# A first store in three transfers, a new list of slots, and one product that signals differently

## The chip, the cores and the metric

The kernel runs on one core of one Trainium2 chip. The metric is the device time of one execution in microseconds (us), given as the median of several runs. Beside it stands one profiled execution, with its own time and its span (from the first to the last instruction of the program).

## What is computed

The input `x` holds 4096 rows of 32 fields of 64 numbers (f32), and `W` is a 64 x 64 matrix. Each field is multiplied by `W`, and then each of the 496 pairs of fields i < j gives one product, number by number:

```python
vid = jnp.einsum('bfd,de->bfe', x, W)
idx_i, idx_j = jnp.triu_indices(F_, k=1)
return x[:, idx_i, :] * vid[:, idx_j, :]
```

So 33.6 MB are read and 4096 x 496 x 64 x 4 B = 520.1 MB are written.

## The kernel before

**Layout.** The two halves of the batch lie side by side on the 128 partitions (2 x 64 numbers of a field), so that a "unit" is one field or one product of a tile: 128 columns of 4 B, that is 512 B on each of 128 partitions, 64 KB in all. The batch is cut into 16 tiles of 128 columns; a tile has 32 fields (units) and 496 products (units). All units live in one SBUF tensor `mem` of 445 units. The output is a stream of 16 x 496 = 7936 products, in an order that `by_block` fixes.

**Work of a tile.** TensorE multiplies the fields by `W` (kept twice on the diagonal of `w2`) into PSUM (`vid`), in two halves of 16 fields: the high half (fields 16 to 31) first, then the low half (`half`, L305). VectorE (DVE) multiplies fields from `mem` with fields from `vid` and writes products back into `mem` (L285): first the pairs within the high half (64 + 32 + 16 + 8 products), then the 256 pairs across the halves, then those within the low half.

**Slots.** `SLOTS` cuts the stream into stores by hand. Each entry is (number of products, first unit in `mem`, seams): the products of a slot lie in consecutive units and leave in one DMA (`store`, L245, through `transfer`, L183, all issued by SyncE, SP). A seam is a place at which a product instruction is cut too, so that a part of a slot can be made before the rest of its units is free. `products` cuts the instructions at slots and seams. A unit may be written again when the store that reads it has landed and the products that read it are made; `after` collects these waits. The homes are so laid that slots reuse the units of older slots and of tiles that are used up. 74 slots make 270 product instructions.

**Loads.** The tiles come in two groups (`GROUPS`): tiles 0 to 7 and tiles 8 to 15. Tile 0 and `W` come first in two loads; then `load(0)` issues three loads of 128, 70 and 26 units. At tile 8, `load(1)` issues three loads of 102, 128 and 26 units over the places of the first group. SP is one queue: what is issued later waits behind what is issued earlier. The first store behind each set of loads also waits until the last but one of these loads has landed (`hold[-2]`). Slots from number `STRETCHES[0]` on are stored behind `load(1)`.

**Signals.** Each product instruction raises one semaphore: `made` (stores and loads wait for it) or `free` (TensorE waits for it before it overwrites a half of `vid`). The last product on a half should raise `free`; if it is the last of its slot it must raise `made`, and a later one raises `free`. For a product that raised `free`, `work` notes the next `made` as the one to wait for, so whoever needs that product waits for one product more.

Of the kernel before, what the change touches and what calls it, by code (L numbers as in the profile page):

```python
# [10 lines left out]
P = 128  # L11
# [10 lines left out]
    (0, [(96, 224), (26, 96), (0, 26)]),  # L22
    (8, [(154, 256), (26, 154), (0, 26)]),
]
STRETCHES = [37]


SLOTS = [
# [10 lines left out]
]  # L39


PAD = 24
# [9 lines left out]
def by_block():  # L52


    def within(lo, fields):
        n, many = fields // 2, 1
        while n:
            yield ((many, fields // many, 0), (n, 0, 1), (n, 1, 1)), lo, lo + fields - 2 * n + 1
            n, many = n // 2, many * 2

    yield from within(16, 16)
    yield ((1, 0, 0), (16, 0, 1), (16, 1, 0)), 0, 16
    yield from within(0, 16)


def products(blocks, at=0):

    for nest, i, j in blocks:
        units = [n for n in accumulate((n for n, _, _ in nest[:0:-1]), lambda a, b: a * b, initial=1)][::-1]
        r, size = 0, units[0] * nest[0][0]  # L70
        while r < size:
            room = min(BREAKS[bisect_right(BREAKS, at)] - at, size - r)
            level = next(k for k, unit in enumerate(units) if r % unit == 0 and room >= unit)
            count = nest[level][0]
            part = min(count - r // units[level] % count, room // units[level])
            places = [r // unit % n for unit, (n, _, _) in zip(units, nest)]
            yield (
                at,
                part * units[level],
                ((part, *nest[level][1:]), *nest[level + 1 :]),  # L80
                i + sum(k * di for k, (_, di, _) in zip(places, nest)),
                j + sum(k * dj for k, (_, _, dj) in zip(places, nest)),
            )
            at += part * units[level]
            r += part * units[level]
# [16 lines left out]
def fields(a, lo, steps, whole):  # L102


    first = a[:, lo : lo + 1, :]
    dims = [[step * C, n] for n, step in steps if n > 1 or whole]
    dims = [*dims[:-1], [1, dims[-1][1] * C]] if whole else [*dims, [1, C]]
    return bass.AP(first.tensor, first.offset, [list(first.ap[0]), *dims])
# [36 lines left out]
def place_of(t, fields):  # L145

    first = max(begin for begin, _ in GROUPS if begin <= t)
    return TOP - (t - first + 1) * fields
# [10 lines left out]
def pairwise_bilinear_kernel(nc, x0, x, out):  # L159
# [8 lines left out]
    mem = ctx.enter_context(nc.sbuf_tensor([P, UNITS, C], F32))  # L168
# [3 lines left out]
    made = nc.alloc_semaphore("made")  # L172
    free = nc.alloc_semaphore("free")
# [3 lines left out]
    sp, dve = Queue(nc.sync, behind), Queue(nc.vector, behind)  # L177
# [3 lines left out]
    def transfer(out_, in_, units, reads, needs):  # L181
        sem = nc.alloc_semaphore(f"moved{len(moved)}")
        sp.issue(lambda: nc.sync.dma_start(out=out_, in_=in_), needs).then_inc(sem, 16)  # L183
        sp.note(sem, 16)
        moved.append((units, reads, sem))
        return sem

    def after(units):

        needs = [(s, 16) for u, reads, s in moved if reads and overlap(u, units)]  # L190
        last = max((n for spans, n in worked if any(overlap(units, s) for s in spans)), default=0)
        return needs + [(made, last)] * (last > 0)

    counts = {made: 0, free: 0}

    def work(make, spans, needs, tells):


        instruction = dve.issue(make, needs)
        instruction.then_inc(tells, 1)  # L200
        counts[tells] += 1
        worked.append((spans, counts[made] + (tells is free)))
        dve.note(tells, counts[tells])
# [18 lines left out]
    owed = 0  # L222
# [3 lines left out]
    def load(g):  # L226
        (begin, pieces), end = GROUPS[g], ends(NT)[g]
        begin = max(begin, 1)
        low = place_of(end - 1, F)
        sems = []  # L230
        for lo, hi in pieces:
            at = (begin - 1) * F + lo - low
            sems.append(transfer(mem[:, lo:hi, :], x[:, at : at + hi - lo, :], (lo, hi), False, after((lo, hi))))
            loads.append((range(begin, end), (lo, hi), sems[-1]))
        return sems

    def loaded(t):
        units = (place_of(t, F), place_of(t, F) + F)
        return [(sem, 16) for tiles, piece, sem in loads if t in tiles and overlap(piece, units)]

    hold = load(0)
    begins = [begin for begin, _ in GROUPS]
    held = []

    def store(slot, last):  # L245
        nonlocal hold
        begin, end = STARTS[slot : slot + 2]
        home = SLOTS[slot][1]
        units = (home, home + end - begin)
        needs = [(made, last)]  # L250
        if hold:
            needs.append((hold[-2], 16))
            hold = []
        transfer(out[:, begin:end, :], mem[:, units[0] : units[1], :], units, True, needs)


    for t in range(NT):
        if t in begins[1:]:
            hold = load(begins.index(t))
            for late in held:  # L260
                store(*late)
            held = []
        xs = (place_of(t, F), place_of(t, F) + F)
        blocks = list(products(by_block(), t * NP))
        for k, (at, n, nest, i, j) in enumerate(blocks):
            slot = bisect_right(STARTS, at) - 1
            begin, end = STARTS[slot], STARTS[slot + 1]
            home = SLOTS[slot][1]
            units = (home + at - begin, home + at - begin + n)
            whole = nest[-1][1:] == (1, 1)  # L270
            inner = [n for n in accumulate((c for c, _, _ in nest[:0:-1]), lambda a, b: a * b, initial=1)][::-1]
            o = fields(mem, units[0], [(c, step) for (c, _, _), step in zip(nest, inner)], whole)
            left = fields(mem, xs[0] + i, [(c, step) for c, step, _ in nest], whole)
            right = fields(vid, j, [(c, step) for c, _, step in nest], whole)
            top = i + sum((c - 1) * step for c, step, _ in nest)
            high = j >= HALF
            later = blocks[k + 1 : k + 2]
            owed += not later or high and later[0][4] < HALF
            tells = free if owed and at + n < end else made
            owed -= tells is free  # L280
            needs = [(there, 2 * t + 2 - high), *after(units)]
            if tells is free and t + 1 < NT and t + 1 not in begins:
                needs += loaded(t + 1)
            work(
                lambda: nc.vector.tensor_tensor(o, left, right, ALU.mult),  # L285
                [units, (xs[0] + i, xs[0] + top + 1)],
                needs,
                tells,
            )
            at += n  # L290
            if at == end:
                late = (slot, counts[made])
                group = sum(behind <= slot for behind in STRETCHES)
                if t < begins[group]:
                    held.append(late)
                else:
                    store(*late)
# [63 lines left out]
```

## Time and profile before

| | |
|---|---|
| Time, median of 3 runs | 1284.66 us (1284.65 to 1284.83) |
| Time of the profiled execution | 1284.39 us |
| Its span | 1283.1 us |
| VectorE busy | 1079.9 us (84%) |
| TensorE busy | 182.7 us (14%) |
| DMA transfers | 8 loads, 74 stores |
| DMA packets | 11,812, 553.71 MB |

The span is 1.3 us shorter than the profiled execution's own time, and that is 0.3 us below the median. Busy shares are averages over the whole span. A DMA "packet" is one piece of a transfer as one of the 16 DMA engines carries it; "landing" is the moment at which the last engine has reported its part. A row of the windows view gives, for a stretch of time, the busy time and the number of instructions of each engine, the granted clock of TensorE, the share of time for which the 16 DMA engines had a packet, and the rate; packets count where they start, so that a short stretch can show more than its share.

### The profile page before, as it was taken

What the parts mean: (1) busy time and instruction counts of PE and PEld (TensorE: products, weight loads), DVE (VectorE), ACT (ScalarE), POOL (GpSimd) and SP (SyncE); (2) the same over time, 40 slices, a digit from 0 to 9 for tenths busy, and PEclk for the clock granted to TensorE, in tenths of its full rate; (3) what the DMA queues carried; (4) which work ended last, traced back from release to release, by engine and by line L of the source; (5) the groups of instructions that cost most, each with busy time, mean ns of one, the idle gap of its engine ahead of it and who ended that gap; (6) DMA issues with size and microseconds to landing.
All of it is one profiled execution on the core that took longest, in us unless ns stands there. A gap on an engine that the chain in (4) does not pass through costs nothing. (4 is left out here: it accounts for less than half of the span.)

```text
span 1283.1 us, 1255 instructions
## 1 busy us (share of the span) xinstructions
PE 182.7 (14%) x256; PEld 71.2 (6%) x256; DVE 1079.9 (84%) x273; POOL 0.2 (0%) x4
## 2 busy tenths in 40 slices
PE   3011120301221030300030112203030020201100
PEld 1000000100000010100010000001010010000000
DVE  5589989988897989998028989989998899899980
POOL 0000000000000000000000000000000000000000
PEclk8566565656556565655565665556565565756655
DMA  9999999999999999999999999999999999999999
GB/s 403 438 429 429 447 421 433 447 427 425 439 444 425 435 427 444 426 431 452 412 426 434 431 431 434 437 433 429 444 431 425 442 437 429 425 435 445 429 423 409
DMA packets 11812, 553.71 MB, mean 432 GB/s; under 512 B 1313, under 2 KB 1313, under 8 KB 1313
## 3 DMA queue, kind: packets, MB, share of 16 engines
q1 hardware_dynamic: 11808, 553.69, 100.0%
q14 instruction: 4, 0.02, 0.0%
HBM read 33.59 MB, written 520.09 MB: 432 GB/s over the span
## 5 line engine op out<-in xcount | busy, mean ns | idle before, releaser
L285 DVE TENSOR_TENSOR mem<-mem,vid 128x1024 f32<-128x1024 f32 (+11 forms) x270 | 1079.3, 4065 | 161.4 <-DMA out_dram<-mem 112.0
L305 PE MATMUL vid<-mem,w 128*128 x256 | 182.7, 881 | 1012.4 <-PEq L303 1012.4
L305 PEld LDWEIGHTS vid<-mem,w 128*128 128x128 f32 x256 | 71.2, 292 | 1123.1 <-issue 1123.1
L217 DVE COPY w<-mem 64x64 f32<-64x64 f32 x2 | 0.4, 189 | 5.2 <-DMA mem<-in_r_x_dram 5.2
L214 DVE MEMSET w<- 128x128 f32 x1 | 0.2, 165 | 0.8 <-PEq L330 0.8
L330 POOL MEMSET const-bfloat16-1.0<- 128x1 bf16 x1 | 0.1, 101 | 0.0
L330 POOL MEMSET const-uint8-127<- 128x1 uint8 x1 | 0.1, 101 | 0.0
L330 POOL MEMSET const-float32-0.0<- 128x1 f32 x1 | 0.1, 98 | 0.2 <-issue 0.2
L330 POOL MEMSET const-float32-1.0<- 128x1 f32 x1 | 0.1, 98 | 0.0
## 6 DMA issues: line engine op xcount, KB each, us to landing
out_dram<-mem SPq DMA_DIRECT2D x12, 7680.0 KB, 23.3
out_dram<-mem SPq DMA_DIRECT2D x5, 7168.0 KB, 22.0
out_dram<-mem SPq DMA_DIRECT2D x4, 6656.0 KB, 20.2
out_dram<-mem SPq DMA_DIRECT2D x6, 4096.0 KB, 17.5
out_dram<-mem SPq DMA_DIRECT2D x4, 5120.0 KB, 19.3
out_dram<-mem SPq DMA_DIRECT2D x3, 6144.0 KB, 20.3
out_dram<-mem SPq DMA_DIRECT2D x3, 5632.0 KB, 18.4
out_dram<-mem SPq DMA_DIRECT2D x2, 5440.0 KB, 19.6
```

The lines of the kernel that those rows point to most:

```text
L214: work(lambda: nc.vector.memset(w2[:, :], 0.0), [], [], made)
L217: lambda: nc.vector.tensor_copy(w2[half, half], mem[half, place + F, :D]),
L285: lambda: nc.vector.tensor_tensor(o, left, right, ALU.mult),
L305: last = nc.tensor.matmul(vid[:, b : b + BANK, :], lhsT=w2[:, :], rhs=xt(b), start=True, stop=True)
L330: nc = _bacc.Bacc("TRN2", target_bir_lowering=False, num_devices=1, dynamic_dma_scratch_size=512)
```

## The change

`SLOTS` is replaced: 75 slots in place of 74, all with new sizes and homes, and the first 38 (not 37) are stored ahead of `load(1)`. Slot 0 now has 28 products, and `PARTS` cuts its store by partitions: rows 0 to 111, 112 to 119 and 120 to 127 go in three transfers. The last product of tile 7, the last one ahead of the second group, now always raises `made`; an instruction of VectorE's sequencer behind it waits for that and raises `free`, so that the loads of the second group wait for this product and not for the next.

```diff
--- before.py
+++ after.py
@@ -22,21 +22,24 @@
     (0, [(96, 224), (26, 96), (0, 26)]),
     (8, [(154, 256), (26, 154), (0, 26)]),
 ]
-STRETCHES = [37]
+STRETCHES = [38]
 
 
 SLOTS = [
-    (80, 256), (109, 336), (83, 240, 16), (56, 323, 13), (64, 379), (80, 240), (56, 323), (64, 379),
-    (104, 224, 99), (117, 328, 51), (115, 208, 16), (96, 323, 5), (64, 192, 16), (88, 256, 67), (96, 344),
-    (112, 192, 64), (128, 304, 40), (128, 160, 32), (128, 288, 16), (128, 144, 16), (120, 272, 16), (80, 128, 16),
-    (104, 208, 64), (128, 312), (128, 112), (128, 240, 72), (128, 96), (128, 224, 16), (112, 80), (120, 192, 32),
-    (120, 312), (128, 48), (128, 176), (128, 304), (128, 32), (128, 160), (128, 304), (104, 256), (85, 360),
-    (51, 240, 16), (64, 291), (88, 355), (104, 240, 51), (88, 344, 11), (72, 224), (64, 296, 48), (85, 360),
-    (107, 224, 72), (112, 331, 29), (120, 192, 32), (120, 312, 19), (112, 176, 16), (64, 288, 24), (80, 352),
-    (128, 176), (128, 304, 48), (128, 144, 32), (128, 272), (120, 128, 16), (120, 248, 24), (96, 112, 16),
-    (112, 208, 40), (120, 320), (120, 112, 96), (128, 232, 88), (128, 80, 32), (128, 208, 24), (128, 48, 32),
-    (128, 176, 32), (120, 304), (120, 48), (128, 168), (128, 296), (120, 48),
+    (28, 256), (68, 284), (92, 352), (108, 240, 16, 44), (88, 348, 4), (60, 240), (68, 300), (76, 368), (76, 224),
+    (64, 300), (80, 364), (104, 224), (112, 328, 36), (120, 192), (116, 312, 16), (108, 176, 16), (64, 284, 28),
+    (96, 348), (128, 176), (128, 304, 44), (120, 144, 32), (128, 264, 40), (88, 128), (112, 216, 48), (112, 328),
+    (128, 128), (128, 256), (128, 80, 48), (128, 208, 48), (104, 336), (128, 80), (120, 208), (128, 48, 32),
+    (128, 176, 32), (128, 304), (128, 16), (128, 144), (116, 272), (100, 256), (88, 356), (52, 240, 16),
+    (76, 292, 64), (77, 368), (99, 240), (104, 339, 29), (72, 224), (80, 296, 43), (64, 376), (104, 224, 72),
+    (112, 328, 48), (120, 192), (116, 312, 16), (108, 176, 16), (96, 284, 28), (64, 380), (128, 176, 108),
+    (128, 304, 76), (120, 144, 32), (128, 264, 40), (88, 128), (112, 216, 48), (112, 328), (128, 112), (128, 240),
+    (128, 80, 32), (128, 208, 32), (104, 336), (128, 80), (120, 208), (128, 48, 32), (128, 176, 32), (128, 304),
+    (128, 16), (128, 144), (120, 272),
 ]
+
+
+PARTS = {0: [slice(0, 112), slice(112, 120), slice(120, 128)]}
 
 
 PAD = 24
@@ -251,7 +254,8 @@
         if hold:
             needs.append((hold[-2], 16))
             hold = []
-        transfer(out[:, begin:end, :], mem[:, units[0] : units[1], :], units, True, needs)
+        for rows in PARTS.get(slot, [slice(0, P)]):
+            transfer(out[rows, begin:end, :], mem[rows, units[0] : units[1], :], units, True, needs)
 
 
     for t in range(NT):
@@ -276,7 +280,8 @@
             high = j >= HALF
             later = blocks[k + 1 : k + 2]
             owed += not later or high and later[0][4] < HALF
-            tells = free if owed and at + n < end else made
+            last = not later and t + 1 in begins
+            tells = free if owed and at + n < end and not last else made
             owed -= tells is free
             needs = [(there, 2 * t + 2 - high), *after(units)]
             if tells is free and t + 1 < NT and t + 1 not in begins:
@@ -287,6 +292,11 @@
                 needs,
                 tells,
             )
+            if last:
+                nc.vector.wait_ge(made, counts[made]).then_inc(free, 1)
+                dve.learn({made.num: counts[made]})
+                counts[free] += 1
+                owed -= 1
             at += n
             if at == end:
                 late = (slot, counts[made])
```

## The prediction

> **What bounds the kernel now.** I read the page first: the span, the busy shares and the DMA rows.
>
> ```profile
> span 1283.1 us, 1255 instructions
> ## 1 busy us (share of the span) xinstructions
> PE 182.7 (14%) x256; PEld 71.2 (6%) x256; DVE 1079.9 (84%) x273; POOL 0.2 (0%) x4
> ...
> DMA packets 11812, 553.71 MB, mean 432 GB/s; under 512 B 1313, under 2 KB 1313, under 8 KB 1313
> ## 3 DMA queue, kind: packets, MB, share of 16 engines
> q1 hardware_dynamic: 11808, 553.69, 100.0%
> ```
>
> The 16 DMA engines hold a packet for 100.0% of the span, and the bytes are those of the input and the output (33.6 and 520.1 MB), so none can be saved. VectorE, at 84%, has slack. The packets tell how a transfer is dealt out. There are 82 transfers (8 loads, 74 stores); 1,312 of the small packets are 82 x 16, a completion from each of the 16 engines; the 10,496 large ones are 82 x 128, one for each partition row. So an engine carries 8 rows of a 128-row transfer.
>
> Then the windows view, by stage (columns: stretch and length; busy time and instructions of PE, PEld, DVE, POOL; granted clock; DMA share, GB/s), to see where time is not spent at full rate.
>
> ```profile
> 0.00:2.00 2.00, 0.00 (x0) 0.00 (x0) 0.17 (x1) 0.20 (x4) 1.00 0.41 59
> ```
>
> ```profile
> 2.00:42.00 40.00, 9.76 (x16) 3.93 (x16) 28.38 (x11) 0.00 (x0) 0.72 1.01 429
> 42.00:642.00 600.00, 82.08 (x112) 31.87 (x112) 511.53 (x126) 0.00 (x0) 0.56 1.00 433
> 642.00:682.00 40.00, 9.93 (x16) 4.05 (x16) 16.71 (x5) 0.00 (x0) 0.59 0.98 424
> 682.00:1282.00 600.00, 80.95 (x112) 31.34 (x112) 523.07 (x131) 0.00 (x0) 0.57 1.00 433
> ```
>
> Both long stretches of stores run at 433 GB/s, share 1.00: a plateau. 553.69 MB at 433 GB/s are 1278.7 us; the span holds 4.4 us more. The first 2 us move 0.12 MB, which loses 1.7 us; 40 us of loading at 429 lose 40 x 4/433 = 0.4 us; the second loading at 424 loses 40 x 9/433 = 0.8 us (a packet at an edge of these 40 us makes both figures rough); the remaining 1.5 us lie in rounding and in the tail. The first 2 us and the final report stay, so **all that any schedule could win is the two losses at the loads and part of the tail, under 2 us of 1283**. Being over 0.2% (2.6 us; about what a measurement of this kernel can tell from no change) faster is all but excluded. Being slower is not: the DMA queue may run dry.
>
> Last the waits, the chain and the timeline, for how near it comes to that.
>
> Who waited for whom (us in total, times, longest), SP's queue and VectorE:
>
> ```profile
> SPq L183 <- DVE mem L285: 1160.2, 74, 50.4
> ```
>
> ```profile
> DVE mem L285 <- DMA out_dram<-mem: 112.0, 35, 18.1
> ```
>
> The chain that ended last (start, length), and the timeline of VectorE behind the store at 737.11:
>
> ```profile
> 665.29 13.03 DVE mem L285 x2
> ...
> 737.11 19.68 DMA out_dram<-mem
> ```
>
> ```profile
> 741.09 12.75 DVE L285 TENSOR_TENSOR mem<-mem,vid 128x640 f32<-128x640 f32 x4 [2.41 <-DMA out_dram<-mem]
> ```
>
> Every store waits for a product, and 35 products wait for a landing that frees their units. The number that matters is the **lead**: landing of the transfer ahead minus issue of the next. The store issued at 737.11 has 741.09 - 737.11 = 4.0 us, and the stretch around it is at 433 GB/s. So 4 us is enough.
>
> **The change, part by part.** Durations first, from the groups by form (count, busy us, mean ns of one).
>
> ```profile
> L285 DVE TENSOR_TENSOR mem<-mem,vid 128x8192 f32<-128x8192 f32 x16 | 138.9, 8680 | 53.3 <-PE vid L305 49.2 <-DMA out_dram<-mem 4.2
> L285 DVE TENSOR_TENSOR mem<-mem,vid 128x2048 f32<-128x2048 f32 x59 | 134.2, 2279 | 10.3 <-DMA out_dram<-mem 10.2
> ...
> L285 DVE TENSOR_TENSOR mem<-mem,vid 128x12288 f32<-128x12288 f32 x7 | 90.7, 12950 | 6.4 <-DMA out_dram<-mem 6.4
> ```
>
> VectorE at the start, SP at the first stores, SP at the second loads, and the last of these loads (KB, us to landing):
>
> ```profile
> 13.59 28.00 DVE L285 TENSOR_TENSOR mem<-mem,vid 128x8192 f32<-128x8192 f32 x9 [7.01 <-PE vid L305]
> 55.32 11.07 DVE L285 TENSOR_TENSOR mem<-mem,vid 128x1408 f32<-128x1408 f32 x5 [13.73 <-DMA out_dram<-mem]
> 71.75 28.74 DVE L285 TENSOR_TENSOR mem<-mem,vid 128x1408 f32<-128x1408 f32 x8 [5.35 <-DMA out_dram<-mem]
> ```
>
> ```profile
> 38.59 1.11 SPq L183 DMA_DIRECT2D out_dram<-mem  x2
> ```
>
> ```profile
> 674.00 0.33 SPq L183 DMA_DIRECT2D mem<-in_r_x_dram  x1
> 678.33 0.34 SPq L183 DMA_DIRECT2D out_dram<-mem  x1
> ```
>
> ```profile
> mem<-in_r_x_dram SPq DMA_DIRECT2D x1, 1664.0 KB, 7.8
> ```
>
> (8680 - 2279) / 48 products = 133 ns a product and 0.146 us an instruction; back to back, nine instructions with 205 products take 28.00 us, so about 0.07 us of the 0.146 remain. A product of 65,536 B takes the DMA 0.1514 us at 433 GB/s.
>
> 1. *New slots.* One slot more is 85 transfers, not 82. What a transfer costs beyond its bytes no row shows alone, so I bound it by two stretches of 200 us with 240 and 160 completions (15 and 10 transfers):
>
> 80 to 280 us, then 420 to 620 us:
>
> ```profile
> DMA packets 2126, 86.91 MB, mean 435 GB/s; under 512 B 240, under 2 KB 240, under 8 KB 240
> ```
>
> ```profile
> DMA packets 1517, 86.84 MB, mean 434 GB/s; under 512 B 160, under 2 KB 160, under 8 KB 160
> ```
>
> Five transfers more move no less. One GB/s (0.5 us in 200) in five is the bound: at most 0.1 us each, 0 to 0.3 us for three. I take +0.1, since the rows are nearer to nothing. VectorE's count of instructions stays near 270, and it has slack.
>
> 2. *Leads.* I walked the new list slot by slot with the two rates above: a product waits until the store that holds its units has landed; meanwhile the queue holds the stores behind that one. The same walk over the old list gives its leads (4.1 for the store at 737.11). Of the new list, the tightest: *Slot 14* needs, after slot 12 lands, 96 + 4 products, 12.95 + 0.6 us, while slot 13 occupies the DMA for 120 x 0.1514 = 18.2 us: lead 4.6. *Slot 44*: 3 + 40 + 32 products, 10.3 us, against slot 43's 99 x 0.1514 = 15.0: 4.7. Slots 23, 51 and 60 come out alike. *Slot 3*, at the start: slots 0 and 1 hold 96 products where the first store held 80, so they land 16 x 0.1514 = 2.4 us after 55.3, at 57.7; 64 products (8.7 us) follow, issue at 66.4; slot 2 lands at 188 products, where 189 landed at 71.7: lead 5.2. *Slot 38*, first behind the second loads: 96 of its products belong to tile 8, as were 96 of the old slot's (3964 products lie ahead of it, 3960 before), so it is issued as far behind its load as the store at 678.33, whose lead was 674.00 + 7.8 - 678.33 = 3.5 us. No slot is below the old list's tightest; I cost the list at 0. If this cover is gone, each us that a lead lacks is a us of idle DMA.
>
> 3. *Loads one product earlier.* The 26-unit load was issued at 674.00, when tile 8's first product (8.68 us from 665.29) was made; now it goes out right behind the 128-unit load, near 622.7. Two rows of SP tell what that is worth, the issue of the other two loads and the 128-unit one's time to landing:
>
> ```profile
> 621.93 1.65 SPq L183 DMA_DIRECT2D mem<-in_r_x_dram  x2
> ```
>
> ```profile
> mem<-in_r_x_dram SPq DMA_DIRECT2D x1, 55.1
> ```
>
> It was under way until about 677.4, past 674.00, and each DMA engine takes its packets in order. So the 26-unit load lands when it did; only if some engines stood idle before its issue does it gain, at most the 0.8 us lost there. I take 0. The wait added on VectorE's queue has behind it only tile 8's products, which stand idle 42 us for the load anyway.
>
> 4. *First store in three.* SP issues two transfers more, about 0.4 us each (two issues took 1.11 us from 38.59 with a wait between them); slot 1 goes out near 40.2, while slot 0 alone gives the engines 28 x 0.1514 = 4.2 us of work: hidden. A row of slot 0 is 28 x 512 = 14,336 B, and an engine moves 433/16 = 27.1 GB/s: 0.53 us. 112 rows are seven for each engine. How 8 rows are dealt no run here shows. Bounds: one row each on eight engines, or all on one. I take the first, as the 128 rows were dealt evenly. If both small transfers go to the same eight, those carry nine rows and the others seven: +0.53 and -0.53 us against before. The work is the same in sum; engines are shifted.
>
> [...] No run here shows a transfer of 8 rows.
>
> Does a shift of 0.53 us live to the end? Completions in short windows tell how far engines are apart:
>
> 52.9 to 54.1 and 54.1 to 55.0 us (the first store):
>
> ```profile
> DMA packets 28, 0.83 MB, mean 695 GB/s; under 512 B 12, under 2 KB 12, under 8 KB 12
> ```
>
> ```profile
> DMA packets 8, 0.22 MB, mean 248 GB/s; under 512 B 4, under 2 KB 4, under 8 KB 4
> ```
>
> 620.85 to 621.55:
>
> ```profile
> DMA packets 32, 1.05 MB, mean 1498 GB/s; under 512 B 16, under 2 KB 16, under 8 KB 16
> ```
>
> 1281.6 to 1282.1 and 1282.1 to 1282.6 (the last store):
>
> ```profile
> DMA packets 7, 0.00 MB, mean 0 GB/s; under 512 B 7, under 2 KB 7, under 8 KB 7
> ```
>
> ```profile
> DMA packets 9, 0.00 MB, mean 0 GB/s; under 512 B 9, under 2 KB 9, under 8 KB 9
> ```
>
> The first store's completions lie from 52.9 to 55.0 us: twelve engines by 54.1, four after. At 621 all sixteen lie within 0.7 us (620.85 to 621.55); the last store's, 7 and 9, within 1281.6 to 1282.6. So a spread made at the start shrinks, and another is made at the second loads. I take it as absorbed: 0.
>
> Sum: +0.1 + 0 + 0 + 0, so 1284.5 for an execution like the profiled one (1284.39), and on the median 1284.66 + 0.1 = **1284.8 us**. Its own range is 1284.4 to 1285.2.
>
> **The rivals.**
> - *The shift lives on* and adds to the engines that end last: +0.53 + 0.1, 1285.3. For: nothing but an empty queue lets a late engine catch up. Against: the spread that shrank by 621. 0.12.
> - *The loads lose less*: four late engines relieved at the first store, no gap at the second loads; at most 0.4 + 0.8 - 0.1 us, 1283.6. For: the 0.98 share. Against: the first store was in the queue from 38.59, before the loads ended at 42 to 43. 0.18.
> - *Slot 38 is late* for the seven-row engines, by up to 1.07 us of its 3.5 (VectorE waits for the late engines, the early ones drain sooner): up to +0.5 in mean, 1285.3. 0.04.
> - *Slower: the 8 rows go to one engine.* 8 x 0.53 = 4.2 us each. On two engines, each is 7 + 8 - 8 = 7 rows late, 3.7 us; on one, 7 + 16 - 8 = 15 rows, 8.0 us. Each landing waits for the late engine; once its lag passes the 4 us of the leads less what issue needs, the others run dry and the program ends with it: 1288.4 to 1292.7. Against: even dealing in all 82 transfers seen. 0.06. [...]
> - *Slower: a slot runs dry* that my walk judged wrong, by some 3 us: 1287.8. 0.03.
>
> **How the numbers follow.** Forecast 0.57, rivals 0.12, 0.18, 0.04, 0.06, 0.03. Only the last two pass +0.2% (1287.2): slower 0.09. The full price of the second rival is still within 0.2%; I leave 0.01 for faster, and 0.90 for the same. The range takes the forecast, the first and the third rival and all but the outermost part of the second: 1283.7 to 1285.6.
>
> **What would show it.** In the profile after: share 100.0% of the queue, plateau rows again 433 GB/s (step 1); a lead of about 4 us at slots 14 and 44 and 3.5 at slot 38 (step 2); the 26-unit load issued near 623 and landing as before near 682 (step 3); 8-row transfers with 8 large packets, and completions near 46 us split into two halves about 1 us apart, but again within 1 us of each other by 621 (step 4). I am wrong if a landing comes 4 us behind its neighbours, or if a long stretch falls below 432 GB/s.

## The result

The changed kernel takes **1289.28 us** (median of 6 runs, 1288.88 to 1289.71) against 1284.66 us before (six runs beside it, 1284.25 to 1284.92): ratio 1.0036, 95% interval 1.0023 to 1.0049, so 4.6 us slower. The forecast was 1284.8 with a range up to 1285.6; the time lies outside it, on the side that had a chance of 0.09. The profiled execution took 1288.88 us, its span is 1287.6 us.

### The profile page after: what moved, and what is told of

It is laid out like the page before. It is cut to its first block, busy times and chain, and to the rows that moved or that the text cites. A ratio compares the mean times of both kernels' runs of the same rounds, so it can differ in the third digit from the quotient of the medians.

```text
span 1287.6 us, 1253 instructions
## 1 busy us (share of the span) xinstructions
PE 182.9 (14%) x256; PEld 71.2 (6%) x256; DVE 1079.6 (84%) x267; POOL 0.2 (0%) x4
## 2 busy tenths in 40 slices
DMA packets 11971, 553.71 MB, mean 430 GB/s; under 512 B 1344, under 2 KB 1344, under 8 KB 1344
## 3 DMA queue, kind: packets, MB, share of 16 engines
q1 hardware_dynamic: 11968, 553.69, 99.9%
## 4 chain that ended last, share of the span: by engine, by line
DVE 53%; DMA 36%; another core or an unknown queue 4%; issue 3%; PE 0%; SPq 0%; DVEq 0%
DVE mem L290 53%; DMA out_dram<-mem 36%; PE vid L315 0%; SPq L186 0%; DVEq L141 0%; SPq L141 0%
## 5 line engine op out<-in xcount | busy, mean ns | idle before, releaser
L290 DVE TENSOR_TENSOR mem<-mem,vid 128x2048 f32<-128x2048 f32 (+14 forms) x264 | 1079.0, 4155 | 168.5 <-DMA out_dram<-mem 121.1
```

## The profile after

The page of the changed kernel, the lines that answer to those of before:

```profile
span 1287.6 us, 1253 instructions
...
PE 182.9 (14%) x256; PEld 71.2 (6%) x256; DVE 1079.6 (84%) x267; POOL 0.2 (0%) x4
...
q1 hardware_dynamic: 11968, 553.69, 99.9%
```

The bytes are the same and the engines still hold a packet nearly always. Nothing here says where 4.5 us went: the DMA is as busy as before (99.9% and 100.0%), but moves less in the time (430 and 432 GB/s over the span). Its windows, by stage:

```profile
2.00:42.00 40.00, 9.76 (x16) 3.92 (x16) 28.37 (x13) 0.00 (x0) 0.71 1.00 420
42.00:92.00 50.00, 5.82 (x8) 2.28 (x8) 25.07 (x8) 0.00 (x0) 0.51 1.01 423
92.00:642.00 550.00, 73.87 (x105) 28.70 (x104) 486.49 (x113) 0.00 (x0) 0.57 1.00 433
642.00:692.00 50.00, 8.51 (x16) 3.51 (x16) 22.16 (x5) 0.00 (x0) 0.60 0.96 410
692.00:1282.00 590.00, 84.95 (x112) 32.80 (x112) 517.33 (x129) 0.00 (x0) 0.55 1.00 433
```

The two long plateaus are at 433 GB/s again. The places that lack are the first 50 us of stores (423, share 1.01: the engines held packets, but the packets were slow) and the second loads (410, share 0.96: some engines held none). A row of 50 us is rough, since packets count where they start; run 1 below has the same rows without the loss. VectorE's timeline at the start shows whom it waited for:

```profile
51.21 3.95 DVE L290 TENSOR_TENSOR mem<-mem,vid 128x1536 f32<-128x1536 f32 x2 [9.91 <-DMA out_dram<-mem]
61.43 9.28 DVE L290 TENSOR_TENSOR mem<-mem,vid 128x8192 f32<-128x8192 f32 x2 [6.27 <-DMA out_dram<-mem]
75.33 11.48 DVE L290 TENSOR_TENSOR mem<-mem,vid 128x1536 f32<-128x1536 f32 x3 [4.62 <-DMA out_dram<-mem]
91.65 7.62 DVE L290 TENSOR_TENSOR mem<-mem,vid 128x7168 f32<-128x7168 f32 x1 [4.83 <-DMA out_dram<-mem]
```

Each of these products starts as a store lands: slots 0, 1, 2 and 3 in this order. Slot 1 was forecast to land at 57.7 us, and lands at 61.4. How far the engines are apart, from the completions (packets under 512 B) of slot 1 in windows 55.7 to 57.7, 57.7 to 59.4 and 59.4 to 61.4 us:

```profile
DMA packets 32, 0.95 MB, mean 473 GB/s; under 512 B 8, under 2 KB 8, under 8 KB 8
```

```profile
DMA packets 22, 0.77 MB, mean 455 GB/s; under 512 B 4, under 2 KB 4, under 8 KB 4
```

```profile
DMA packets 24, 0.92 MB, mean 459 GB/s; under 512 B 4, under 2 KB 4, under 8 KB 4
```

Eight engines are done by 57.7, the other eight are up to 3.7 us later. So half of the engines are late, as they would be if the same eight took both 8-row transfers (had each taken one of them, all sixteen would be about equally late), and by far more than the two rows of 0.53 us between nine and seven. The trace's records of single packets, which the views do not print, show the slow ones: of the 128 packets of slot 0 (14,336 B each) 20 took longer than 0.6 us, up to 3.3 us. In the kernel of run 1 all 128 took 0.54 us.

## The experiments

The runs are numbered. **Theory P (place).** Rows that lie side by side share a way, and engines that carry such rows at the same time hold each other up. Eight engines with eight neighbouring rows would take four times as long for a row, 2.1 us in place of 0.53 (an estimate: two such rows in place of one are 3.7 us late, as slot 1 is). In a transfer of 128 rows, at 0.53 us a row, they would not meet. **Rivals:** L, the new list leaves the DMA dry somewhere; S, a small transfer has a fixed price whatever its rows; K, only transfers on fewer than 16 engines are slow. Each diff below is against the changed kernel unless it says otherwise.

**1. Slot 0 in one transfer.**

```diff
-PARTS = {0: [slice(0, 112), slice(112, 120), slice(120, 128)]}
+PARTS = {}
```

> The changed kernel with slot 0 in one transfer of 128 rows again; new list and earlier loads stay. In the changed kernel slot 0's last piece landed at 51.2 us, some 4 us behind its turn, and the last landing of every later store stays 3.7 to 4.9 us behind that of the kernel before. Theory P (place): eight engines that read rows 112 to 119 (then 120 to 127) at once share one or two ways out of SBUF, so that a row of 14,336 B takes about 2.1 us, not 0.53; the late engines never catch up, and the list and the loads cost nothing. Rival L (list): the new slots leave the DMA dry somewhere. P: 1284.7 us (1284.3 to 1285.2), slot 0 landed by 48. L: over 1287.

Measured: 1284.61 us, ratio to the kernel before 0.9999 (0.9990 to 1.0008). The same rows of VectorE's timeline:

```profile
47.52 3.95 DVE L290 TENSOR_TENSOR mem<-mem,vid 128x1536 f32<-128x1536 f32 x2 [7.11 <-DMA out_dram<-mem]
57.78 9.29 DVE L290 TENSOR_TENSOR mem<-mem,vid 128x8192 f32<-128x8192 f32 x2 [6.30 <-DMA out_dram<-mem]
71.69 11.48 DVE L290 TENSOR_TENSOR mem<-mem,vid 128x1536 f32<-128x1536 f32 x3 [4.62 <-DMA out_dram<-mem]
88.01 7.62 DVE L290 TENSOR_TENSOR mem<-mem,vid 128x7168 f32<-128x7168 f32 x1 [4.84 <-DMA out_dram<-mem]
```

Slot 0 lands at 47.5, not 51.2, slot 1 at 57.8 (forecast 57.7). Its windows for the first 50 us of stores and for the second loads, 439 and 425 GB/s where the changed kernel has 423 and 410:

```profile
42.00:92.00 50.00, 5.17 (x8) 2.08 (x8) 28.71 (x8) 0.00 (x0) 0.56 1.01 439
642.00:692.00 50.00, 10.08 (x16) 4.04 (x16) 25.49 (x6) 0.00 (x0) 0.57 0.99 425
```

**The whole loss comes from the cut in three; L is out.** The list and the earlier loads cost and win nothing that these runs tell.

**2. The loads alone**, on the kernel before:

```diff
-            tells = free if owed and at + n < end else made
+            last = not later and t + 1 in begins
+            tells = free if owed and at + n < end and not last else made
...
+            if last:
+                nc.vector.wait_ge(made, counts[made]).then_inc(free, 1)
...
```

> The kernel before with nothing of the change but the last product of tile 7 raising made, so that the 26-unit load is issued some 51 us earlier. Prediction step 3: nothing, 1284.4 to 1284.7 (within 0.3 us of the kernel before); at most 0.8 us better if engines stood idle before that load.

Measured: 1284.41 us, ratio 1.0000 (0.9991 to 1.0009). As expected, nothing.

**3. Ten transfers alone**, behind the last landing of the kernel before:

```diff
...
+    for rows in AGAIN:
+        sem = transfer(out[rows, begin:end, :], mem[rows, units[0] : units[1], :], units, True, [])
+        nc.sync.wait_ge(sem, 16)
```

> The kernel before, and behind its last landing ten transfers one by one, each waiting for the one ahead: they store rows of the last slot (61,440 B each) once more. Rows: 0 to 127; 112 to 127; 112 to 119; every fourth of 96 to 124; every sixteenth of 0 to 112; 112 to 115; every fourth of 112 to 124; every 32nd of 0 to 96; 0 to 63; every second of 0 to 126. Alone a row takes 2.27 us (its packets at the end of the kernel before). [...] Rival S (fixed cost of a small transfer): by rows to an engine, 8, 1, 1, 1, 1, 1, 1, 1, 4, 4: 18.2, then 2.3 seven times, 9.1, 9.1. [...]

There is one run of this kernel. SP's timeline gives the ten issues; each comes as the transfer ahead has landed:

```profile
1282.80 0.33 SPq L189 DMA_DIRECT2D out_dram<-mem  x1
```

```profile
1302.36 0.34 SPq L189 DMA_DIRECT2D out_dram<-mem  x1
```

```profile
1313.27 0.33 SPq L189 DMA_DIRECT2D out_dram<-mem  x1
```

```profile
1324.02 0.79 SPq L189 DMA_DIRECT2D out_dram<-mem  x1
```

```profile
1328.15 0.59 SPq L189 DMA_DIRECT2D out_dram<-mem  x1
```

```profile
1334.55 0.26 SPq L189 DMA_DIRECT2D out_dram<-mem  x1
```

```profile
1345.24 0.63 SPq L189 DMA_DIRECT2D out_dram<-mem  x1
```

```profile
1349.23 0.51 SPq L189 DMA_DIRECT2D out_dram<-mem  x1
```

```profile
1355.55 0.51 SPq L189 DMA_DIRECT2D out_dram<-mem  x1
```

```profile
1376.39 0.50 SPq L189 DMA_DIRECT2D out_dram<-mem  x1
```

`AGAIN` holds the ten choices of rows that the table below lists. And the last one's issue to landing (KB, us):

```profile
out_dram<-mem SPq DMA_DIRECT2D x1, 3840.0 KB, 10.8
```

In the table, a step runs from one issue to the next, and for the last transfer from issue to landing. The third column is read off the steps: a whole number of rows of 2.27 us, the time of a row at the end of the kernel before, and their sum in us. The last is what such a sum leaves of the step.

| rows | step, us | rows of 2.27 us | what is left, us |
|---|---|---|---|
| 0 to 127 | 19.6 | 8: 18.2 | 1.4 |
| 112 to 127 | 10.9 | 4: 9.1 | 1.8 |
| 112 to 119 | 10.8 | 4: 9.1 | 1.7 |
| 96, 100, ... 124 | 4.1 | 1: 2.3 | 1.8 |
| 0, 16, ... 112 | 6.4 | 2: 4.5 | 1.9 |
| 112 to 115 | 10.7 | 4: 9.1 | 1.6 |
| 112, 116, 120, 124 | 4.0 | 1: 2.3 | 1.7 |
| 0, 32, 64, 96 | 6.3 | 2: 4.5 | 1.8 |
| 0 to 63 | 20.8 | 8: 18.2 | 2.6 |
| 0, 2, ... 126 | 10.8 | 4: 9.1 | 1.7 |

A fixed 1.4 to 2.6 us is left in all ten. S gives 2.3 us for the seven behind the first and is out, and so is K, by the 10.9 us of rows 112 to 127 on sixteen engines. Eight neighbouring rows cost as much as sixteen, and the same number of rows four apart a quarter (9.1 and 2.3 us; the steps with the fixed part are 10.8 and 4.1): this is theory P's four to one. Rows 0, 32, 64 and 96, the farthest apart, cost more than four rows that are four apart (6.3 and 4.0 us): it is not distance that counts. Steps of 10.7 to 10.9 us belong to 4, 8 and 16 neighbouring rows, 6.3 and 6.4 to rows 32 and 16 apart, 4.0 and 4.1 to rows four apart; beyond these choices no run shows which rows share a way. Each of these transfers changes the rows read in SBUF and the rows written in the output together, so no run here parts the two sides, and where the way lies is not shown. The window from 1313.3 to 1323.95 us also shows how many engines carry 8 rows:

```profile
DMA packets 16, 0.49 MB, mean 46 GB/s; under 512 B 8, under 2 KB 8, under 8 KB 8
```

Eight rows and eight completions: eight engines with a row each, as the prediction took it.

**4. The 8 rows as evens and odds**, in the queue, with as many transfers:

```diff
-PARTS = {0: [slice(0, 112), slice(112, 120), slice(120, 128)]}
+PARTS = {0: [slice(0, 112), slice(112, 128, 2), slice(113, 128, 2)]}
```

> The changed kernel with as many transfers, rows and engines, but its two small transfers take rows 112, 114, ... 126 and 113, 115, ... 127. The kernel with rows four apart does not settle it: there SP's issues of the small transfers came 2.3 us apart and slot 1's first only at 46.7 us, when the engines with few rows had run out. Theory P: two rows to a way out, not four: 1.07 us a row instead of 2.1; the late engines' lag falls from 3.7 to about 1.6 us: 1286.2 to 1287.2. Rival S: as the changed kernel, 1289.

```profile
49.33 3.95 DVE L290 TENSOR_TENSOR mem<-mem,vid 128x1536 f32<-128x1536 f32 x2 [7.59 <-DMA out_dram<-mem]
59.58 9.29 DVE L290 TENSOR_TENSOR mem<-mem,vid 128x8192 f32<-128x8192 f32 x2 [6.30 <-DMA out_dram<-mem]
```

Against one transfer, slots 0 and 1 land 1.8 us later (49.33 - 47.52, 59.58 - 57.78), where P said 1.6 and S 3.7. So P holds here in the queue too, though SP's issues differ (five in 8.67 us, against 4.80 in the changed kernel). But the total is 1288.21 us, ratio 1.0028 (1.0017 to 1.0039), over P's range, which ended at 1287.2: something is added later.

**5. One transfer of 16 rows in place of two of 8.**

```diff
+PARTS = {0: [slice(0, 112), slice(112, 128)]}
```

> Slot 0 in two transfers, rows 0 to 111 and 112 to 127: every engine carries 8 rows again. Theory P: sixteen engines read 16 neighbouring rows at once, four to a way out, 2.1 us instead of 0.53 on all engines: 1284.7 + 1.6 = 1286.3. Rival K: only transfers on fewer than 16 engines are slow: 1284.7.

Measured: 1286.73 us, ratio 1.0016 (1.0007 to 1.0026). K, which said 1284.7, is out here as well: with 8 rows on every engine (1344 completions for its 84 transfers, 16 each) the kernel is 2.1 us slower than that of run 1. VectorE's timeline:

```profile
48.93 3.95 DVE L290 TENSOR_TENSOR mem<-mem,vid 128x1536 f32<-128x1536 f32 x2 [7.26 <-DMA out_dram<-mem]
```

Slot 0 lands at 48.93 us, 1.4 us behind run 1; P said 1.6. The rest comes later.

**6. Four times 8 rows, together and four apart.**

```diff
+PARTS = {0: [slice(0, 96), slice(96, 104), slice(104, 112), slice(112, 120), slice(120, 128)]}
```

> The changed kernel with slot 0 cut into rows 0 to 95 and four transfers of 8 neighbouring rows. Theory P: the eight engines carry 6 rows of 0.53 us and 4 of 2.1 us, 11.8 us where 8 rows took 4.3: 7.5 us late, 1284.7 + 7.5 + up to 0.8 = 1292 to 1293. Rival S (small transfers): each small transfer costs its engines a fixed 1.5 us whichever rows it has: 4 x 1.5 + 1.1 = 7 us, 1292. Rival L: as the changed kernel, 1289 to 1290.

```diff
+PARTS = {0: [slice(0, 96), slice(96, 128, 4), slice(97, 128, 4), slice(98, 128, 4), slice(99, 128, 4)]}
```

> The same bytes, engines and number of transfers as the kernel with four transfers of 8 neighbouring rows, but each takes every fourth row: 96, 100, ... 124, then 97, 101, ... and so on. Theory P: rows four apart do not share a way out, so each row takes 0.53 us again; eight engines carry 10 rows, the others 6: +1.1 us, 1285.3 to 1286.0. Rival S: the cost is that of small transfers, 1292. Rival L: 1289 to 1290.

Measured: 1289.17 us (ratio 1.0035, 1.0023 to 1.0047) and 1287.83 us (1.0022, 1.0013 to 1.0032). The landing of slot 0, together and apart:

```profile
50.45 3.95 DVE L290 TENSOR_TENSOR mem<-mem,vid 128x1536 f32<-128x1536 f32 x2 [9.00 <-DMA out_dram<-mem]
```

```profile
48.89 3.95 DVE L290 TENSOR_TENSOR mem<-mem,vid 128x1536 f32<-128x1536 f32 x2 [8.32 <-DMA out_dram<-mem]
```

Rows apart are cheaper, so P has the sign right, but neither size fits: in total together is 3 us less than P said, apart 2 us more. At slot 0 together is 2.9 us late where P said 7.5, even less than the changed kernel's two small transfers (3.7); apart is 1.4 late where P said 1.1. SP's queue shows why this is no clean test; its seven issues of stores from 38 us on, rows apart:

```profile
38.27 9.00 SPq L186 DMA_DIRECT2D out_dram<-mem  x7
```

Seven issues took 9.0 us, and 10.4 with rows together (three took 1.34 us with one transfer). Slot 1's stood behind four small ones, and the engines that had only six rows ran out ahead of it (DMA share from 38 to 50 us: 92.3% together, 97.8% apart, 102.9% with one transfer). That is a price of cutting up a store which the prediction did not have. Why four transfers of neighbouring rows crowd less than two is open; their issues lie further apart, and by the packet records the longest packet of slot 0 took 1.7 us, not 3.3.

**7. A later slot cut**, slot 25 with 128 products, first in 112, 8 and 8 rows, then in 96 and four times 8 rows four apart.

```diff
+PARTS = {25: [slice(0, 112), slice(112, 120), slice(120, 128)]}
```

```diff
+PARTS = {25: [slice(0, 96), slice(96, 128, 4), slice(97, 128, 4), slice(98, 128, 4), slice(99, 128, 4)]}
```

> Slot 0 in one transfer, and slot 25 (128 products, 65,536 B a row, stores alone in the queue) cut in rows 0 to 111, 112 to 119, 120 to 127. Theory P: the price grows with the bytes: a row takes 2.42 us, four to one way out 9.7 us; the eight engines carry 7 x 2.42 + 2 x 9.7 = 36.3 us in place of 19.4: 17 us late; 1297 to 1302. Rival S (fixed 1.5 us a small transfer): 2 x 1.5 + 2.4 = 5.4 us, 1288 to 1290.

> Slot 25 again, now rows 0 to 95 and four transfers of rows four apart. The kernel with slot 25 in 112, 8 and 8 rows took 1315.4 us, 31 us more, where theory P said 12 to 17. Theory P with owners (a late small transfer also shares its ways with the engines that serve these rows in the next store): rows four apart have one small reader and at most one owner to a way, so a row takes 2.4 to 4.8 us: eight engines carry 6 + 4 rows, 24.2 us, up to 33.8, in place of 19.4: 4.8 to 14.4 us late, 1289 to 1299. Rival O (the order in the queue, not the rows): four small transfers cost more than two, over 1315.

Measured: 1315.44 us (ratio 1.0238, 1.0222 to 1.0254) and 1308.38 us (1.0184, 1.0168 to 1.0199). The cut costs 31 us where the row is 65,536 B and 4.6 us where it is 14,336 B: the price grows with the bytes, and S is out a second time. So is O, which had the second kernel over 1315. But both sizes exceed P's by far: 31 us where P said 12 to 17, 24 where it said 5 to 14. Windows of the first:

```profile
392.00:452.00 60.00, 6.26 (x8) 2.36 (x8) 27.39 (x7) 0.00 (x0) 0.53 0.90 272
452.00:480.00 28.00, 0.00 (x0) 0.00 (x0) 26.02 (x4) 0.00 (x0) 0.50 0.88 379
```

At share 0.90 the DMA moves 272 GB/s for 60 us: packets that hold an engine but move slowly. P counted the small transfers alone, with 9.7 us a row. The packet records of the first kernel show more: from 390 to 416 us 24 packets of 65,536 B took over 3.9 us (with one transfer, 2.42), and behind them thirteen took 11.3 to 16.9 us. If a packet's time tells how many share a way, up to seven did (16.9/2.42), and part of the large transfer was slow too. Why the price is over P's is not shown. A guess of the author's, which no run separates: a late engine also holds up the engine that carries the neighbouring rows in the next store.

**8. The part that comes later.** In the kernels of 4 and 5 the lag behind the kernel with one transfer grows after the first stores, with no small transfer left. Here slot 0 is one transfer, and slot 3's store waits once for slot 2's landing:

```diff
+PARTS = {}
...
+        if slot == 3:
+            needs.append((moved[-1][2], 16))
```

> Slot 0 in one transfer, and slot 3's store alone waits also for slot 2's landing, so that all 16 engines run dry once, near 71 us, for about 2.3 us, and start again together. It is for the part of the changed kernel's loss that comes after the first stores: the lag behind the kernel with one transfer grows from 3.7 us at 72 us to 4.3 us at the end, and with evens and odds from 1.8 to 2.9 us, with no slot 0 left in the queue. Theory D (step): engines that have been thrown out of their order take 0.1 to 0.2% longer per packet from there, so the lag grows from some 2.3 us at 88 us to 3.0 to 3.5 us at 640 us; total 1287.4 to 1288.2. Rival N: the gap is all, 2.3 us at every slot, 1286.7 to 1287.1.

Measured: 1287.76 us, ratio 1.0024 (1.0015 to 1.0033). VectorE's timeline, where slot 3 has landed and where the last product of tile 7 waits for a store, of this kernel and of the one with one transfer:

```profile
89.94 7.62 DVE L292 TENSOR_TENSOR mem<-mem,vid 128x7168 f32<-128x7168 f32 x1 [6.31 <-DMA out_dram<-mem]
...
628.14 0.69 DVE L292 TENSOR_TENSOR mem<-mem,vid 128x512 f32<-128x512 f32 x1 [16.26 <-DMA out_dram<-mem]
```

```profile
624.71 0.69 DVE L290 TENSOR_TENSOR mem<-mem,vid 128x512 f32<-128x512 f32 x1 [16.16 <-DMA out_dram<-mem]
```

The lag is 1.9 us at 88 us (89.94 - 88.01) and 3.4 at 625 (628.14 - 624.71): a gap in the first stores grows by 1.5 us without any further one. In the changed kernel it grows from 3.6 (91.65 - 88.01) to 4.4, with evens and odds from 1.8 to 2.6. So N is out, and the effect that D names (longer packets) is there. The windows cannot show it (433 GB/s on both sides, and 1 GB/s would be 1.3 us in 550); the packet records can. From 92 to 625 us a packet takes 37.849 ns per KB in run 1's kernel, 37.918 here and 37.906 in the changed kernel: 0.18% and 0.15% longer, which is 1.0 and 0.8 us in 533. These are single executions. Why packets take longer after such a gap or delay stays open.

No kernel here beats the one before: one transfer with the new list (0.9999) and the loads alone (1.0000) equal it.

## Why the prediction was wrong

**Step 4 failed, at "A row of slot 0 is 28 x 512 = 14,336 B, and an engine moves 433/16 = 27.1 GB/s: 0.53 us".** Eight engines with one row each was right (run 3). But 27.1 GB/s was read from 128-row transfers; with 8 neighbouring rows the engines hold each other up (run 3: steps of 10.8 us together, 4.1 four apart, or 9.1 and 2.3 without the fixed part). By P a row then takes 4 x 0.53 = 2.1 us, an estimate; the sixteen longest packets of slot 0 took 1.9 us on average. Two rows at 2.1 in place of one at 0.53 are 3.7 us late, and slot 0 landed 51.21 - 47.52 = 3.7 us late.

**"I take it as absorbed: 0" failed too.** The completions of the store that lands at 629 us, from 625.6 to 626.0 and from 626.0 to 628.9 us:

```profile
DMA packets 18, 0.61 MB, mean 1516 GB/s; under 512 B 8, under 2 KB 8, under 8 KB 8
```

```profile
DMA packets 28, 1.19 MB, mean 412 GB/s; under 512 B 8, under 2 KB 8, under 8 KB 8
```

Eight engines are still some 3 us behind the other eight, where the prediction had them within 1 us by 621. The spread has shrunk since slot 1, but the late engines have made up nothing: it is the early ones that have fallen back. A reason is that VectorE can only make the next store once the late engines have landed; how much of the shrinking that explains, no row shows. The late engines have no gap in which to catch up (DMA share 1.00 from 92 to 642 us). The first rival (0.12) was right in kind. At the second loads the early engines' waiting shows as share 0.96 and 410 GB/s; the lead at slot 38 ran short, as the third rival said, but at the cost of the early engines alone. The product of tile 7 that waits for a store, in the changed kernel:

```profile
629.10 0.69 DVE L290 TENSOR_TENSOR mem<-mem,vid 128x512 f32<-128x512 f32 x1 [16.27 <-DMA out_dram<-mem]
```

It is 4.4 us behind run 1 (624.71) ahead of these loads, and the span is 4.5 us behind (1287.6 and 1283.1).

The fourth rival had the size, 3.7 us, by coincidence, with another mechanism: rows heaped on one or two engines. What heaps up, by theory P, is not rows on an engine but engines on a way. Its chance of 0.06 was argued down by "even dealing in all 82 transfers seen"; that dealing is even in rows was true and beside the point.

Right were: by run 1, step 1 (75 slots, plateau 433 GB/s again, 1284.61 us against the forecast 1284.8) and step 2 (slot 1 landed at 57.78 for 57.7 forecast; the list costs nothing), step 3 (run 2 gives 1.0000; by the packet records before, the 26-unit load, issued at 674.00, starts its packets of 13,312 B at 676.2 us, behind the 128-unit load's last one of 65,536 B at 674.9), and, as far as these runs go, that 0.2% is not to be won: none of them was faster than before.

Of the 4.6 us, 3.7 are slot 0's late landing, by run 1 the work of the cut; about 0.7 come between 92 and 625 us, of the kind of run 8, whose cause is open; the rest is within the spread of the runs.

## What to carry to other kernels

A rate per engine taken from 128-row transfers did not hold for 8 neighbouring rows (0.53 us a row forecast, 1.9 us on average for the sixteen longest packets): before a store is cut by partitions, ask which rows are read at the same time and whether they hold each other up (run 3: 9.1 us for eight side by side, 2.3 for eight that are four apart). In a queue with no gap (DMA share 1.00 from 92 to 642 us) the delay of some engines was not made up (3.7 us at slot 1, 4.4 at 629 us), and the others ended up waiting for them. Transfers run alone behind the last landing (run 3) show which rows crowd each other, but not the price in the queue: that was under half of what P worked out in run 6 (rows together, at slot 0) and about twice as much in run 7.

## What the runs showed of the hardware

Neighbouring rows hold each other up: transfers of one row of 61,440 B an engine took 10.7 to 10.9 us with 4, 8 or 16 rows side by side, 6.3 and 6.4 with rows 32 and 16 apart and 4.0 and 4.1 with rows four apart, some 1.7 us of each fixed; rows 0 to 63 took as long as all 128 (20.8 and 19.6 us). Small transfers are also slow to issue behind others: seven issues in 9.0 us, three in 1.34. And after one gap of some 2 us on all engines, near 71 us, the lag grew by 1.5 us more by 625 us.
